# Smaller pieces for the adjacency loads and a new order of the drain in a fused graph-attention layer

## The chip, the core and the metric

The kernel runs on one core of one Trainium2 chip. The metric is the time of the whole program on the device in microseconds (us). Most executions of one kernel lie within about 1 us of its median here; the "span" in a profile is the time from the first to the last recorded instruction of one execution and is about 2 us shorter than the time of that execution on the device.

Engine names in the profile: PE is TensorE (matrix products), PEld its weight loads, DVE VectorE, ACT ScalarE, POOL GpSimd, SP SyncE. The granted clock is the share of its full clock that TensorE had, 1.00 being full; the DMA share is the mean busy share of the core's 16 DMA engines. A "q" behind a name (POOLq, SPq) marks an instruction of that engine's sequencer: a wait, a branch, the issue of a DMA.

## The reference, cut to what matters

One graph-attention layer over 4096 nodes with 4 heads, a residual and a layer norm:

```python
ht  = (x @ W).reshape(N, 4, 512).transpose(1, 0, 2)
e   = leaky_relu(src[:, :, None] + dst[:, None, :], 0.01) + adj[None]
att = softmax(e, axis=-1)
x   = layernorm(x + mean_over_heads(att @ ht))
```

The values of `adj` run up to 1e9, so in nearly every row the softmax puts all its weight on the column of the row's largest `adj`. The kernel uses this: it finds that column, gathers that row of `x`, multiplies it by the mean of the heads' weights, adds the residual and normalises. It also counts the rows in which the largest value does not lead by enough (a bound on the attention logits decides). If the count, the "flag", is not zero, a general path runs. Here it is zero, but every engine must load the flag and branch on it at the end.

## The kernel before

The 4096 rows are 32 blocks of 128 rows. A block passes these stages: load 2 MB of `adj`; largest value of each 64-column segment on VectorE; best segment, gather of it (`lead`), column within it; gather of the rows of `x` (`y`); turning (four transposes) on TensorE, a copy on ScalarE (`yt`), four products with `w_sum`; statistics on ScalarE (the reciprocal of the deviation on GpSimd) and scaling on ScalarE. In the profiles each of the four products, and a residual, shows as two matmul records (x8, x2), and the four transposes of a turning as x4. In the code below, `...` marks what is cut.

```python
def load_adj(ib):                       # SyncE's queue
    ...
    n = PIECES if ib in (0, NB - 1) else 1          # PIECES = 4
    for k in range(n):
        nc.sync.dma_start(t[:, ts(k, N // n)], adj_rows[ib][:, ts(k, N // n)])

def segment_maxima(ib, lo, hi):
    ...
    n = PIECES if ib in (0, NB - 1) else 2
    for k in range(lo * n // PIECES, hi * n // PIECES):
        nc.vector.tensor_reduce(seg_of[ib][:, ts(k, S // n)], adj_t[ib][:, ts(k, N // n)]..., op=OP.max)
```

The end of the program, the "drain", by its calls (the stores on SyncE's queue are cut; `LAST_X` is 28, `NB` 32, `FINISH` 6):

```python
find_column(NB - 2)
find_column_in_row(NB - 1)              # search over 4096 columns, then gather of row 31
rstd(slice(NB - FINISH, NB - FINISH + 2))   # GpSimd: statistics of blocks 26, 27
...
project(NB - 3, residual=False)         # turn 29, copy, four products
finish(NB - FINISH); finish(NB - FINISH + 1)
for ib in range(LAST_X, NB):
    row_norm(ib)                        # ScalarE: squares of blocks 28..31
finish_last(NB - 4, True)
find_inner(NB - 1)
bound(0)                                # largest square; TensorE turns that column
project(NB - 2, residual=False)
finish_last(NB - 3, True)
bound(1)
project(NB - 1)
finish_last(NB - 2, True)
bound(2); test(); pg = count()
finish_last(NB - 1, False)
store(nc.scalar, NB - 1, 1)
report(pg)                              # writes the flag
```

Each engine runs its instructions in this order. `finish_last` is a chain of VectorE instructions, with one small ScalarE instruction in it, over a block of 128 x 512.

## Time and profile before

| | before |
|---|---|
| time, median (lowest to highest) | 258.02 us (257.52 to 258.42) |
| span of the profiled run | 255.2 us |
| all DMA engines full | until about 236 us |
| VectorE through with block 31 of adj | 218.58 us |
| products of block 28 start | 220.22 us |
| last row of the result ready | 247.78 us |
| flag ready | 248.13 us |

The page's first part gives busy time, share of the span and number of instructions of each engine; the line of GB/s gives what the DMA engines moved in each of 40 equal slices (6.4 us each):

```profile
PE 206.2 (81%) x677; PEld 104.4 (41%) x678; DVE 188.9 (74%) x298; ACT 110.1 (43%) x266; POOL 97.5 (38%) x213
GB/s 245 433 419 424 412 420 419 429 409 411 434 414 410 417 424 417 416 419 417 414 428 406 426 409 424 417 415 412 426 412 422 413 399 403 392 379 397 47 48 46
```

No compute engine is busy all the time, and the DMA moves some 415 GB/s through nearly all slices but stops three slices before the end. Thus two limits follow one another: the loads, and a tail of dependent work.

### The profile page before, as it was taken

What the parts mean: (1) busy time and instruction counts of PE and PEld (TensorE: products, weight loads), DVE (VectorE), ACT (ScalarE), POOL (GpSimd) and SP (SyncE); (2) the same over time, 40 slices, a digit from 0 to 9 for tenths busy, and PEclk for the clock granted to TensorE, in tenths of its full rate; (3) what the DMA queues carried; (4) which work ended last, traced back from release to release, by engine and by line L of the source; (5) the groups of instructions that cost most, each with busy time, mean ns of one, the idle gap of its engine ahead of it and who ended that gap; (6) DMA issues with size and microseconds to landing.
All of it is one profiled execution on the core that took longest, in us unless ns stands there. A gap on an engine that the chain in (4) does not pass through costs nothing.

```text
span 255.2 us, 2524 instructions
## 1 busy us (share of the span) xinstructions
PE 206.2 (81%) x677; PEld 104.4 (41%) x678; DVE 188.9 (74%) x298; ACT 110.1 (43%) x266; POOL 97.5 (38%) x213
## 2 busy tenths in 40 slices
PE   0189958999999999999795979694999699684940
PEld 0035426555556665565342434242344244241410
DVE  2536686595999599959897998599959999737350
ACT  2012004044646575757481638190558182825100
POOL 1112323245445544553444445534554455530000
PEclk9999799599999999999998899998699999898895
DMA  7999999999999999999999999999999999999111
GB/s 245 433 419 424 412 420 419 429 409 411 434 414 410 417 424 417 416 419 417 414 428 406 426 409 424 417 415 412 426 412 422 413 399 403 392 379 397 47 48 46
DMA packets 15428, 97.76 MB, mean 383 GB/s; under 512 B 2344, under 2 KB 2344, under 8 KB 10032
## 3 DMA queue, kind: packets, MB, share of 16 engines
q1 hardware_dynamic: 11664, 87.82, 83.8%
q0 software_dynamic: 3584, 9.44, 9.5%
q10 hardware_dynamic: 160, 0.28, 0.3%
q8 instruction: 7, 0.11, 0.2%
q14 instruction: 13, 0.11, 0.1%
HBM read 89.15 MB, written 8.39 MB: 382 GB/s over the span
## 4 chain that ended last, share of the span: by engine, by line
DMA 32%; POOL 19%; issue 19%; PE 15%; DVE 7%; ACT 3%; SPq 1%; POOLq 0%; DVEq 0%
DMA adj_t<-in_adj_dram 14%; DMA hold<-in_x_dram 12%; PE o L211 10%; POOL y L174 6%; POOL lead L164 6%; DVE seg L151 4%; DMA hold<-in_L_gnn_W_dram 4%; DMA lead<-in_adj_dram,row 3%; POOL sd L229 3%; PE o L207 2%; POOL row L162 1%; PE pv L281 1%; ACT sq L218 1%; POOL start L169 1%; ACT hold L234 1%
## 5 line engine op out<-in xcount | busy, mean ns | idle before, releaser
L151 DVE TENSOR_REDUCE seg<-adj_t 128x32 f32<-128x2048 f32 (+1 forms) x68 | 145.9, 2150 | 36.6 <-DMA adj_t<-in_adj_dram 35.9
L211 PE MATMUL o<-w_sum,yt 128*128 128x512 f32 x256 | 125.0, 633 | 2.3 <-ACT yt L205 2.3
L211 PEld LDWEIGHTS o<-w_sum,yt 128*128 128x128 f32 x256 | 49.3, 202 | 65.3 <-issue 51.5
L174 POOL DMA_INDIRECT y<-in_x_dram,col x32 | 32.1, 1003 | 19.3 <-POOL col L187 15.5
L205 ACT COPY yt<-tp 128x512 f32<-128x512 f32 x32 | 18.8, 586 | 46.3 <-PE tp L203 46.3
L164 POOL DMA_INDIRECT lead<-in_adj_dram,row x32 | 31.0, 968 | 15.5 <-POOL row L162 15.5
L207 PE MATMUL o<-hold,ident 128*128 128x512 f32 x58 | 32.5, 645 | 0.8 <-DMA hold<-in_x_dram 0.8
L257 PE MATMUL o<-hold,ident 128*128 128x512 f32 x32 | 18.4, 726 | 16.9 <-DMA hold<-in_L_gnn_W_dram 16.9
L203 PE MATMUL tp<-ident,y 128*128 128x128 f32 x128 | 20.2, 282 | 13.9 <-DMA y<-in_x_dram,col 13.7
L203 PEld LDWEIGHTS tp<-ident,y 128*128 128x128 f32 x128 | 14.9, 144 | 25.9 <-issue 25.9
L162 POOL TENSOR_TENSOR row<-at,first 128x1 uint32<-128x1 uint32 x32 | 5.9, 184 | 50.9 <-DVE at L160 49.7
L234 ACT ACTIVATE hold<-o,nm,sd 128x512 f32<-128x512 f32 x28 | 20.3, 780 | 10.9 <-POOL nm L230 10.9
L275 ACT COPY wt<-tp 128x512 f32<-128x512 f32 x16 | 9.2, 587 | 35.4 <-PE tp L273 35.4
L187 POOL TENSOR_TENSOR col<-start,within 128x1 uint32<-128x1 uint32 x31 | 5.8, 188 | 40.4 <-DVE within L185 38.1
L281 PEld LDWEIGHTS pv<-at_d,wt 128*128 128x128 f32 x128 | 17.2, 200 | 7.4 <-ACT wt L275 3.7
L218 ACT ACTIVATE sq<-hold 128x512 f32<-128x512 f32 x32 | 19.8, 619 | 0.0
L225 ACT ACTIVATE sq<-o,nm 128x512 f32<-128x512 f32 x28 | 19.2, 688 | 0.9
L257 PEld LDWEIGHTS o<-hold,ident 128*128 128x128 f32 x32 | 7.2, 237 | 25.4 <-POOL row L162 11.6
L223 ACT ACTIVATE sq<-o 128x512 f32<-128x512 f32 x28 | 16.9, 605 | 0.0
L258 ACT ACTIVATE w_sum<-o 128x512 f32<-128x512 f32 x4 | 2.4, 598 | 33.0 <-PE o L257 33.0
L281 PE MATMUL pv<-at_d,wt 128*128 128x2 f32 x128 | 16.0, 249 | 0.6 <-ACT wt L275 0.6
L273 PEld LDWEIGHTS tp<-ident,hold 128*128 128x128 f32 x64 | 7.9, 142 | 6.9 <-issue 6.9
(73 smaller groups left out, 117.2 us busy)
## 6 DMA issues: line engine op xcount, KB each, us to landing
adj_t<-in_adj_dram SPq DMA_DIRECT2D x30, 2048.0 KB, 32.1
hold<-in_x_dram SPq DMA_DIRECT2D x8, 1024.0 KB, 33.2
out_dram<-hold SPq DMA_DIRECT2D x31, 256.0 KB, 5.2
adj_t<-in_adj_dram SPq DMA_DIRECT2D x8, 512.0 KB, 6.7
hold<-in_L_gnn_W_dram SPq DMA_DIRECT2D x4, 1024.0 KB, 18.0
lead<-in_adj_dram,row POOLq DMA_INDIRECT x32, 6.7
y<-in_x_dram,col POOLq DMA_INDIRECT x32, 8.3
out_dram<-hold ACTq DMA_DIRECT2D x1, 256.0 KB, 2.1
```

What stands on the lines that cost most here:

```text
L151: nc.vector.tensor_reduce(seg_of[ib][:, ts(k, S // n)], adj_t[ib][:, ts(k, N // n)].rearrange("p (s e) -> p s e", e=E), axis=AX.X, op=OP.max,)
L164: nc.gpsimd.indirect_dma_start(out=lead, out_offset=None, in_=adj_segs, in_offset=bass.IndirectOffsetOnAxis(ap=row[:, :1], axis=0),)
L174: nc.gpsimd.indirect_dma_start(out=y, out_offset=None, in_=x, in_offset=bass.IndirectOffsetOnAxis(ap=col[:, :1], axis=0),)
L203: nc.tensor.transpose(tp[:, kb, :], y[:, ts(kb, P)], ident)
L205: nc.scalar.copy(yt, tp)
L207: nc.tensor.matmul(o, ident, hold[:, ib, :], start=True, stop=False)
L211: nc.tensor.matmul(o, yt[:, kb, :], w_sum[:, kb, :], start=(kb == 0 and not residual), stop=(kb == KB - 1),)
L218: nc.scalar.activation(sq, hold[:, ib, :], AF.Square, accum_out=xx[:, ib : ib + 1])
L225: nc.scalar.activation(sq, o, AF.Square, bias=nm[:, i], accum_out=sd[:, i])
L234: nc.scalar.activation(hold[:, ib, :], o_ps.pop(ib), AF.Identity, bias=nm[:, i], scale=sd[:, i])
L257: nc.tensor.matmul(o, ident, hold[:, w_at + kb * H + h, :], start=(h == 0), stop=(h == H - 1))
L281: nc.tensor.matmul(pv[:, kb, h : 2 * H : H], wt[:, k, :], at_d[:, k, h : 2 * H : H], start=(k == 0), stop=(k == KB - 1),)
```

## The change

Its intent: let VectorE start on half a block instead of waiting for a whole one, and shorten the tail by giving each engine's queue an order in which nothing stands behind a wait that it does not need. The diff, cut to its core:

```diff
+    LATE = NB - Q
+    def pieces(ib):
+        return PIECES if ib == 0 or ib >= LATE else PIECES // 2
     def load_adj(ib):
-            n = PIECES if ib in (0, NB - 1) else 1
+            n = pieces(ib)
     def segment_maxima(ib, lo, hi):
-        n = PIECES if ib in (0, NB - 1) else 2
+        n = pieces(ib)
 ... (project() becomes turn(), residual(), products(ib, lo, hi); the loop's order is unchanged)
     find_column(NB - 2)
+    rstd(slice(NB - FINISH, NB - FINISH + 2))
     find_column_in_row(NB - 1)
-    rstd(slice(NB - FINISH, NB - FINISH + 2))
-    project(NB - 3, residual=False)
+    turn(NB - 3)
+    products(NB - 3, 0, KB - 1)
     finish(NB - FINISH)
     finish(NB - FINISH + 1)
-    for ib in range(LAST_X, NB):
+    for ib in range(LATE, NB):
         row_norm(ib)
+    turn(NB - 2)
+    products(NB - 3, KB - 1, KB)
+    bound(0)
+    products(NB - 2)
     finish_last(NB - 4, True)
     find_inner(NB - 1)
-    bound(0)
-    project(NB - 2, residual=False)
+    bound(1)
     finish_last(NB - 3, True)
-    bound(1)
-    project(NB - 1)
+    bound(2)
+    test()
+    turn(NB - 1)
+    residual(NB - 1)
+    products(NB - 1, 0, KB - 1)
+    pg = count()
+    products(NB - 1, KB - 1, KB)
     finish_last(NB - 2, True)
-    bound(2)
-    test()
-    pg = count()
+    report(pg)
     finish_last(NB - 1, False)
     store(nc.scalar, NB - 1, 1)
-    report(pg)
```

(The stores on SyncE's queue are cut here; they keep their order. `LATE` is 28, as `LAST_X` was. A DMA packet of adj is one row's part of a piece: 16,384 B for whole blocks, 8,192 for halves, 4,096 for quarters.)

## The prediction

> **What bounds the kernel now.** I read the slices first, then busy times in stretches, then the end in order of time. The stretches (length, busy microseconds of each engine, granted clock, DMA share, GB/s):
>
> ```profile
> 20.00:190.00 170.00, 153.23 (x541) 81.49 (x540) 137.64 (x209) 81.83 (x196) 75.87 (x160) 0.94 1.01 418
> 222.00:236.00 14.00, 9.50 (x25) 4.13 (x24) 7.88 (x13) 5.72 (x16) 2.37 (x5) 0.87 1.03 388
> 236.00:248.20 12.20, 9.60 (x26) 4.08 (x24) 5.95 (x22) 1.38 (x4) 0.00 (x0) 0.92 0.13 47
> 248.20:255.30 7.10, 0.00 (x0) 0.00 (x0) 0.00 (x0) 0.00 (x0) 0.00 (x0) 0.51 0.13 47
> ```
>
> Until 236 us the sixteen DMA engines are full (share 1.01 to 1.03) and set the pace. Then come 12 us with DMA nearly idle, in which TensorE works 9.6 us, and 7 us in which no engine computes. So there are three terms: when VectorE is through with the last block of adj (set by DMA), the drain from there to the last row, and the exit.
>
> Term one. VectorE waits for adj 35.9 us in all, and in the timeline starts a block when the whole of it has landed:
>
> ```profile
> 190.12 2.29 DVE L151 TENSOR_REDUCE seg<-adj_t 128x32 f32<-128x2048 f32 x1 [2.49 <-DMA adj_t<-in_adj_dram]
> ...
> 218.36 0.22 DVE L160 FIND_INDEX8 at<-top,seg 128x8 uint32<-128x64 f32 x1
> ```
>
> The trace's landings for blocks 27 to 30 are 190.09, 195.82, 201.41 and 207.20; the reductions start at 190.12, 195.84, 201.43 and 207.23. Block 31 comes in quarters, the last at about 213.3 (worked out from 208.59 for the first and 211.84 for the third). VectorE is one block behind, ending at 218.58.
>
> Term two, from the timeline of the end:
>
> ```profile
> 220.22 5.40 PE L211 MATMUL o<-w_sum,yt 128*128 128x512 f32 x8 [0.97 <-ACT yt L205]
> 226.13 0.94 POOL L174 DMA_INDIRECT y<-in_x_dram,col  x1 [3.81 <-PE tp L203]
> 228.45 1.45 ACT L234 ACTIVATE hold<-o,nm,sd 128x512 f32<-128x512 f32 x2 [1.77 <-POOL nm L230]
> 233.58 0.27 PE L308 MATMUL px<-ident,xm 128*1 128x128 f32 x1 [3.15 <-DVE xm L306]
> 234.98 5.20 PE L211 MATMUL o<-w_sum,yt 128*128 128x512 f32 x8 [0.68 <-ACT yt L205]
> 245.49 0.70 DVE L243 BATCH_NORM_STATS2 st<-o 128x6 f32<-128x512 f32 x1 [1.30 <-PE o L211]
> ```
>
> GpSimd stands at the gather of block 31's row until the 4.42 us search is over, then does the statistics of blocks 26 and 27 behind it; ScalarE finishes those at 228.45 and squares four rows; VectorE takes the largest at 233.36; and TensorE, at whose queue's head stands the turning of that column (the "last factor", the bound), idles 3.15 us. Row 30 had landed at 226.82, so block 30 waits for nothing of its own. After the pause its products take 5.20 us instead of 3.68.
>
> Term three. The last row is written at 247.78, the flag at 248.13, the last record ends at 255.2. The sequencers' records after the flag (count: shortest/median/longest ns, first to last start):
>
> ```profile
> L60 POOLq TENSOR_LOAD <-any_bad x1: 492/492/492, 248.2 to 248.2; - x1
> L61 PEldq COMPARE_BRANCH x2: 95/1834/3574, 248.8 to 249.2; - x2
> L641 POOLq DRAIN x3: 40/107/5307, 249.1 to 254.9; - x3
> ```
>
> All five engines load the flag at 248.2. TensorE's branch then takes 3.57 us (to 252.8), GpSimd's first drain 5.31 us (to 254.4). SyncE waits for the last store (landed at 249.88) and is through at 251.5. So the exit hangs on the flag, not on the store, by about 3 us.
>
> **What the Trainium skill says.** "DMA: Bandwidth & Descriptors", Why small descriptors are slow, gives every packet a fixed overhead of about 3 cycles. The trace agrees in kind: median 621 ns for 16,384 B, 316 for 8,192 B, 164 for 4,096 B (16 KB as 621, 632, 656). Its Anatomy of one DMA has about 2 us of fixed cost, mostly the receipt; the last store took 2.07 us. "TensorE: Matmul & The Clock Gate", What's actually happening: an idle window of about 3.4 us brings the clock to half. The trace's clock records show 0.5 from 234.6 to 238.0, after the 3.15 us pause. "Advanced Engine Details and Errata", Control Flow Timing, puts a compare-and-branch at about 108 ns; one here took 3,574 ns, so the measured one is used.
>
> **The change part by part.**
>
> *adj in halves and quarters.* Bytes are the same. Cost: halves need 8 more packets on each engine in a block (128 rows over 16 engines), and two of 8,192 B take 2 x 316 - 621 = 11 ns more than one of 16,384 B: 8 x 11 = 0.09 us a block, 27 blocks, 2.4 us by the medians. From 20 to 60 us the medians were 619 and 312, giving 8 x 5 ns x 27 = 1.1 us. I take 1.7, and 0.2 more for quarters of block 28 on: adj lands some 1.9 us later. Gain: VectorE has block 27's first half done when the second lands (190.09 + 1.9 = 192.0), ends that block 2.27 + 0.55 us later at 194.8, and then works through four blocks at 5.75 us each (its time for block 31 before, 212.81 to 218.58): 194.8 + 23.0 = 217.8 to 218.0, against 218.58. Quarters land every 1.4 us and take 1.15 us, so VectorE no longer waits for whole blocks. Net: -0.6 us. In flight are now eight pieces of 1 or 0.5 MB instead of whole blocks; each piece waits for the eighth before it. 4 MB at 410 GB/s is 10 us of work, so I expect no hole.
>
> *Drain.* Let T be the start of block 28's products, 220.22 before and 219.6 after.
> - T to T+5.4: products of 28, as slow as before (the clock dropped at 221.0 after waits that stay).
> - Turning and copying 29: T+6.6. Three products at 0.92: T+9.35. Turning 30 (0.6): T+9.95. Fourth product: T+10.85.
> - ScalarE: copy of 29 to T+6.55, blocks 26 and 27 finished (1.45; their statistics now precede the gather on GpSimd) to T+8.0, four squares (2.44) to T+10.45, copy of 30 to T+11.05. VectorE's largest value is there at T+10.65, before TensorE asks: the 3.15 us are gone.
> - Products of 30 at full clock (3.7): T+14.8, against T+19.96 before (240.18). That is 5.2 us.
> - Bound 0.3, turning 31 0.6, copy 0.65, three products 2.75, count 0.2, fourth product 0.92: T+20.3.
> - VectorE: block 28 from T+10.65 (2.75 us as before), two small ones 0.5, block 29 2.75, factor and test 1.3, block 30 2.75: T+20.7. Report 0.45, flag at T+21.1. Block 31's statistics and scaling 2.3 (245.49 to 247.78): T+23.4.
> Before, the last row stood at T+27.56. The drain gives 4.2 us; VectorE, not TensorE, is then last by 0.7.
>
> *Exit.* Flag T+21.1: GpSimd 0.95 to its drain and 5.3 in it, T+27.35. VectorE needs 3.9 us from its last instruction to its own drain (248.13 to 252.0, load and branch within), T+27.3. Store: 2.1 landing, 0.3, then 1.3 in SyncE: T+27.1. All meet; 0.8 us of closing gives T+28.2. After the last row that is 4.8 instead of 7.4: 2.6 us.
>
> Sum: 0.6 + 4.2 + 2.6 = 7.4 us. 258.02 - 7.4 = 250.6; I put it at 250.8 because the chains meet tightly.
>
> **The rivals.**
> (1) Smaller pieces slow the DMA by more. For: steady means are 627 and 324 ns, which gives 8 x 21 ns x 27 = 4.5 us instead of 1.7. Against: from 20 to 60 us, with 512 packets of 8,192 B among 700 of 16,384 B, the core moved 421 GB/s, more than anywhere else. It would make 253.5.
> (2) GpSimd's long drain or the branches are a fixed tail after the last work, not after the flag. For: the drain stands near the end whatever runs. Against: it starts 0.2 us after its branch, while a store is still out. It would leave 7.4 us of exit: 253.3.
> (3) The clock. Fuller work before 219 us could spare the slow products of 28 (1.6 us): 249.1. Or a new short wait throttles 30 or 31 again: 252.3.
> (4) The eight in flight are too few and leave holes in the DMA. For: the queue shrinks from some 10 to 4 MB. Against: stores of 256 KB, eight in flight, still moved 388 GB/s. It could cost 3 us or more.
> (5) The row gathers gain, since each waits behind shorter packets (8.3 us landing under whole blocks, 6.0 among stores). They are on no path that I found in the middle; up to 1 us in the drain.
>
> **Range and chances.** (1) and (2) are each some one in six and cost about 2.7 us; both together cancel most of the gain. (3) is worth 1.5 us either way. The range is 248.6 to 253.6. Two per cent is 252.86, 2 us above my middle, so faster has 0.8. Slower needs holes: 0.02.
>
> **What would show it.** Right: adj's last landing near 215, VectorE through block 31 by about 218; no wait of TensorE for the largest square; products of 30 near 3.7 us; the flag before the last row; under 5 us from the last row to the end; full DMA to about 238. Wrong: DMA slices under full before 230, a last landing past 217, a wait of over 1 us between the products of 29 and 31, or GpSimd's drain still ending 6 us after the last row.

## The result and the profile after

| | before | after |
|---|---|---|
| time, median of the first job | 257.77 us (4 runs) | 249.25 us (4 runs, 248.82 to 250.11) |
| ratio | | 0.9673, 95% interval 0.9635 to 0.9711 |
| span | 255.2 us | 246.9 us |

A ratio here is the mean time of one kernel's fast runs over that of the other's of the same rounds, so it is not quite the ratio of the medians. In the experiments the profiled run counts in the medians and not in the ratio; in the first job it counts in both.

The stretches of the changed kernel (start:end, length, busy us and number of instructions of PE, PEld, DVE, ACT and POOL, granted clock, DMA share, GB/s); the third ends with the last row:

```profile
20.00:190.00 170.00, 153.81 (x551) 81.01 (x550) 135.87 (x206) 82.08 (x197) 76.39 (x160) 0.96 1.02 412
222.00:236.00 14.00, 13.09 (x41) 5.84 (x40) 8.43 (x20) 6.64 (x18) 2.83 (x5) 1.00 1.04 392
236.00:241.70 5.70, 3.27 (x9) 0.95 (x7) 4.68 (x15) 0.59 (x2) 0.00 (x0) 1.00 0.75 286
241.70:246.90 5.20, 0.00 (x0) 0.00 (x0) 0.00 (x0) 0.00 (x0) 0.00 (x0) 0.60 0.19 65
```

The profile is that of the fastest of the four runs (248.82 us). The first row is the cost: with a DMA share that is still full, 412 GB/s instead of 418. The second is the gain: TensorE works 13.1 of 14 us where it had worked 9.5, at full clock. The stretch after the last row, with no engine computing, is 5.2 us long where it was 7.4.

VectorE's timeline in the changed kernel:

```profile
193.13 2.29 DVE L155 TENSOR_REDUCE seg<-adj_t 128x32 f32<-128x2048 f32 x1 [0.53 <-DMA adj_t<-in_adj_dram]
196.00 2.33 DVE L155 TENSOR_REDUCE seg<-adj_t 128x16 f32<-128x1024 f32 x2
...
219.09 0.23 DVE L164 FIND_INDEX8 at<-top,seg 128x8 uint32<-128x64 f32 x1 [0.29 <-issue]
```

The first line is the second half of block 27. VectorE waited for it, so it landed at 193.13; all of block 27 had landed at 190.09 before. The loads are 3.0 us late by then. From 196.0 on VectorE works without waiting and is through with block 31 at 219.32, 0.74 us later than before. So the earlier start on each block did not make up for the slower loads.

The end, in order of time, for the same instructions as in the prediction:

```profile
220.46 3.70 PE L217 MATMUL o<-w_sum,yt 128*128 128x512 f32 x8 [1.71 <-ACT yt L206]
...
223.80 0.19 POOL L236 TENSOR_TENSOR nm<-nm,sd 128x2 f32<-128x2 f32 x1
...
225.54 1.46 ACT L240 ACTIVATE hold<-o,nm,sd 128x512 f32<-128x512 f32 x2
...
229.70 0.27 PE L314 MATMUL px<-ident,xm 128*1 128x128 f32 x1
...
229.96 3.70 PE L217 MATMUL o<-w_sum,yt 128*128 128x512 f32 x8
...
239.42 0.68 DVE L249 BATCH_NORM_STATS2 st<-o 128x6 f32<-128x512 f32 x1
```

The statistics of blocks 26 and 27 are ready at 223.99 (before, 228.42), ScalarE finishes the two blocks 2.9 us earlier, and the turning of the column of largest squares has no wait in brackets any more. The products of block 30 take 3.70 us and start 5.0 us earlier than before. The products of block 28 also take 3.70 us, where they took 5.40.

The sequencers at the end of the changed kernel:

```profile
L60 POOLq TENSOR_LOAD <-any_bad x1: 503/503/503, 239.5 to 239.5; - x1
L61 PEldq COMPARE_BRANCH  x2: 95/1954/3814, 240.1 to 240.6; - x2
L656 POOLq DRAIN  x3: 40/107/5307, 240.4 to 246.6; - x3
L656 SPq DRAIN  x3: 7/7/7, 246.0 to 246.3; - x3
```

The flag is loaded at 239.5, before the last row is ready (241.69). GpSimd's drain, again 5,307 ns, ends at 245.8, and SyncE, which waits for the last stores, is through at 246.0. The two paths now meet.

### The profile page after: what moved, and what is told of

Its sections match the earlier page's. It is cut to its first block, busy times and chain, and to the rows that moved or that the text cites. A ratio compares the mean times of both kernels' runs of the same rounds, so it can differ in the third digit from the quotient of the medians.

```text
span 246.9 us, 2569 instructions
## 1 busy us (share of the span) xinstructions
PE 201.8 (82%) x677; PEld 101.2 (41%) x678; DVE 188.8 (76%) x304; ACT 109.6 (44%) x266; POOL 97.5 (39%) x213
## 4 chain that ended last, share of the span: by engine, by line
DMA 47%; issue 19%; POOL 19%; DVE 10%; ACT 2%; POOLq 0%; PE 0%; DVEq 0%
DMA adj_t<-in_adj_dram 38%; DMA hold<-in_L_gnn_W_dram 6%; POOL lead L168 6%; POOL y L178 6%; DVE seg L155 4%; DMA y<-in_x_dram,col 3%; POOL sd L235 2%; POOL start L173 1%; POOL row L166 1%; DVE st L249 1%; POOL col L191 1%; DVE hold L255 1%; ACT sq L224 1%; DVE hold L246 1%; POOL sd L234 1%
## 5 line engine op out<-in xcount | busy, mean ns | idle before, releaser
L217 PE MATMUL o<-w_sum,yt 128*128 128x512 f32 x256 | 118.4, 604 | 7.4 <-ACT yt L206 7.4
L217 PEld LDWEIGHTS o<-w_sum,yt 128*128 128x128 f32 x256 | 46.2, 191 | 65.7 <-issue 45.5
L263 PE MATMUL o<-hold,ident 128*128 128x512 f32 x32 | 22.2, 860 | 16.3 <-DMA hold<-in_L_gnn_W_dram 16.3
L210 PE MATMUL o<-hold,ident 128*128 128x512 f32 x58 | 30.6, 610 | 0.0
L204 PE MATMUL tp<-ident,y 128*128 128x128 f32 x128 | 20.2, 281 | 11.3 <-DMA y<-in_x_dram,col 11.2
L263 PEld LDWEIGHTS o<-hold,ident 128*128 128x128 f32 x32 | 8.5, 279 | 27.2 <-POOL row L166 11.5
L287 PEld LDWEIGHTS pv<-at_d,wt 128*128 128x128 f32 x128 | 16.3, 191 | 6.8 <-ACT wt L281 3.7
L287 PE MATMUL pv<-at_d,wt 128*128 128x2 f32 x128 | 15.3, 244 | 0.6 <-ACT wt L281 0.6
```

The lines of the kernel that those rows point to most:

```text
L204: nc.tensor.transpose(tp[:, kb, :], y[:, ts(kb, P)], ident)
L210: nc.tensor.matmul(o_ps[ib], ident, hold[:, ib, :], start=True, stop=False)
L217: nc.tensor.matmul(o_ps[ib], yt_of[ib][:, kb, :], w_sum[:, kb, :], start=(start and kb == 0), stop=(kb == KB - 1),)
L263: nc.tensor.matmul(o, ident, hold[:, w_at + kb * H + h, :], start=(h == 0), stop=(h == H - 1))
L287: nc.tensor.matmul(pv[:, kb, h : 2 * H : H], wt[:, k, :], at_d[:, k, h : 2 * H : H], start=(k == 0), stop=(k == KB - 1),)
```

## The experiments

Three theories had to be told apart. A: the gain is the drain's order and the flag's place, and the smaller pieces give nothing or cost. B: the pieces carry a good part. C, on the exit: it is a fixed tail after the last work. All twelve kernels gave correct results. "Before" ran beside each of them; its median was 257.90, 258.01 and 257.58 us in the three jobs. The jobs ran on different chips (e1 to e4, e5 to e8, and e9 to e12), so runs of different jobs are compared by their ratios.

| run | what | median us | ratio to before, 95% interval |
|---|---|---|---|
| e9 | the changed kernel again | 249.06 | 0.9685 (0.9652 to 0.9717) |
| e1 | before + pieces | 256.37 | 0.9984 (0.9941 to 1.0027) |
| e2 | changed, whole blocks | 247.69 | 0.9610 (0.9587 to 0.9634) |
| e3 | changed, flag last | 251.79 | 0.9776 (0.9747 to 0.9805) |
| e4 | changed, whole to 27, then quarters | 248.70 | 0.9641 (0.9612 to 0.9669) |
| e5 | changed, whole to 23, halves to 27, quarters | 247.27 | 0.9590 (0.9548 to 0.9633) |
| e6 | changed, statistics behind the gather | 252.19 | 0.9791 (0.9747 to 0.9836) |
| e7 | changed, 30 turned after the bound's column | 250.64 | 0.9722 (0.9681 to 0.9763) |
| e8 | e2 + statistics ahead in the whole loop | 247.40 | 0.9608 (0.9560 to 0.9656) |
| e10 | e5 + e8 | 249.83 | 0.9686 (0.9642 to 0.9729) |
| e11 | before + flag early | 256.47 | 0.9951 (0.9923 to 0.9980) |
| e12 | changed, every block in quarters | 254.18 | 0.9866 (0.9829 to 0.9903) |

### e1: the pieces alone

```diff
+    def pieces(ib): return PIECES if ib == 0 or ib >= LATE else PIECES // 2
-            n = PIECES if ib in (0, NB - 1) else 1      # and 2 in segment_maxima
+            n = pieces(ib)
```

> The kernel before with adj in halves and the last four blocks in quarters, nothing else. Theory A (the pieces buy nothing: shorter packets make the last adj land 2.6 us later, 215.4 instead of 212.8, and VectorE ends block 31 at 219.3 instead of 218.6): 257.8 to 258.8 us, ratio 1.000 to 1.004, with the 3.15 us wait of TensorE for the largest square still there. Rival B (the pieces carry a good part of the 8.5 us, by fuller TensorE work and no drop of its clock before the drain): under 256.3 us, with the products of block 28 at 3.7 us instead of 5.4. If only the clock counts and it is luck of the window, the time follows that one group: 1.7 us less where it shows 3.7.

The median was 256.37 us, but the runs spread from 254.85 to 259.24, and the ratio cannot be told from 1. So A's range of times (257.8 to 258.8) was missed, and B's was not reached. That ratio counts two runs that the record marks slow (258.70 and 259.24); the other three of its rounds give 0.994. By the packet records the last adj was in at 215.29, against 212.75 before; VectorE was through with block 31 at 218.68, not at the 219.3 expected. TensorE still waited for the largest square:

```profile
232.68 0.27 PE L312 MATMUL px<-ident,xm 128*1 128x128 f32 x1 [2.37 <-DVE xm L310]
```

Its profiled run (254.85) was the fastest and had the products of blocks 28 and 30 at 3.70 us each, without a drop of the clock. B's limit, 256.3 us, is a ratio of 0.994, just at the interval's lower end, so a gain of about 1.5 us in the old drain, of pieces or of the clock, is not ruled out. It is no large part of 8.5 us.

### e2: the changed kernel with whole blocks

```diff
-            n = pieces(ib)
+            n = PIECES if ib in (0, NB - 1) else 1      # and 2 in segment_maxima
```

> The changed kernel with adj as before (whole blocks, 0 and 31 in quarters). Theory A: 248.2 to 249.3 us, as fast as the changed kernel or up to 1 us faster: last adj back at 212.8, DMA done 2.6 us earlier, block 31 through VectorE at 218.6. Rival B (the pieces carry part of the gain): over 250.5 us.

It was faster than the changed kernel: 247.69 us, and its interval (0.9587 to 0.9634) lies under that of the changed kernel run again (0.9652 to 0.9717). Theory A holds, by somewhat more than its best case. The loads moved as fast as before again:

```profile
20.00:190.00 170.00, 148.53 (x545) 78.41 (x544) 136.86 (x210) 83.03 (x197) 76.58 (x160) 0.98 1.01 418
```

VectorE was through with block 31 at 218.23, the last row stood at 240.70, and the products of 28 began at 219.88:

```profile
219.88 3.70 PE L217 MATMUL o<-w_sum,yt 128*128 128x512 f32 x8 [1.30 <-ACT yt L206]
```

So the pieces cost the changed kernel some 0.75% (0.9685 - 0.9610), or about 1.9 us.

### e3: the flag last

```diff
-    report(pg)
     finish_last(NB - 1, False)
     store(nc.scalar, NB - 1, 1)
+    report(pg)
```

> The changed kernel with the flag reported after the last row, as before. Theory A (the exit hangs on the flag: 1 us to GpSimd's drain, 5.3 us in it): exit from the last row's end back from 5.2 to about 7.4 us, 251.2 to 251.6 us. Rival (the exit is a fixed tail after the last work or store): 249.0 to 249.5 us.

It took 251.79 us, just over A's range, about 0.9% or 2.4 us more than the changed kernel by the ratios (0.9776 - 0.9685). The last row came at 241.85, nearly as in the changed kernel (241.69), but the exit after it took 7.44 us instead of 5.22:

```profile
L60 POOLq TENSOR_LOAD <-any_bad x1: 502/502/502, 242.3 to 242.3; - x1
L656 POOLq DRAIN  x3: 40/107/5307, 243.2 to 249.0; - x3
```

The long drain starts 0.9 us after the flag's load, wherever the flag is, and sets the end. Theory C falls.

### e4: whole blocks, then quarters

```diff
-            n = pieces(ib)
+            n = PIECES if ib == 0 or ib >= LATE else 1
```

> The changed kernel with whole loads for blocks 1 to 27 and quarters for 28 to 31. Theory A: packets of 16,384 B bring the last adj back to about 213.2; but VectorE, which starts block 27 when all of it has landed (190.1) and takes 5.1 us for it and 5.8 us for each block in quarters, still ends at about 218.4: 248.3 to 249.2 us. Rival B: over 250.5 us.

It gave 248.70 us, as A expected, and was no faster than e2 (247.69). The last adj was in at 212.90, VectorE through at 218.48. Whole loads through block 27 restore the DMA, but since block 27 must land whole, VectorE gains nothing from the quarters. In its profiled run the products of block 28 were slow:

```profile
219.81 5.40 PE L217 MATMUL o<-w_sum,yt 128*128 128x512 f32 x8 [2.36 <-ACT sq L224]
```

### e5: whole, then halves, then quarters

```diff
-        return PIECES if ib == 0 or ib >= LATE else PIECES // 2
+        if ib == 0 or ib >= LATE: return PIECES
+        return PIECES // 2 if ib >= LATE - Q else 1
-        n = pieces(ib)                  # in segment_maxima
+        n = max(2, pieces(ib))
```

> The changed kernel with whole loads for blocks 1 to 23, halves for 24 to 27, quarters for 28 to 31. If what the pieces cost is their packets (8 ns each) and what they give is an earlier start of VectorE on the last blocks, both show here: last adj near 213.3 (0.6 us later than with whole blocks), block 31 through VectorE at 216 to 217 instead of 218.2. If the start of block 28's products hung on VectorE, 246.5 to 247.5 us; if it hangs on ScalarE's chain (statistics of 24 and 25, then 26, then the copy of 28), which starts from VectorE's end of block 30, the same, for that comes earlier too. Rival (neither counts): 247.7 as with whole blocks.

It reached 247.27 us, the lowest median of all. The last adj was in at 213.81, and VectorE was through 2.6 us earlier than in the changed kernel:

```profile
190.58 2.29 DVE L157 TENSOR_REDUCE seg<-adj_t 128x32 f32<-128x2048 f32 x1 [0.21 <-DMA adj_t<-in_adj_dram]
...
216.45 0.23 DVE L166 FIND_INDEX8 at<-top,seg 128x8 uint32<-128x64 f32 x1 [0.29 <-issue]
```

Products of 28 began at 217.91 and the last row stood at 239.56, 2.1 us before the changed kernel's. In this profile the pieces pay, since they shorten the wait that lasts to the end. About half a microsecond of it went in a longer exit (5.7 us: SyncE was held by the stores until 243.1, 3.5 us after the last row; in the changed kernel it was 3.0), and the interval overlaps that of e2, so the gain over whole blocks is not certain. It does beat both kernels: its interval ends at 0.9633, that of e9 begins at 0.9652.

### e6: the statistics behind the gather again

```diff
     find_column(NB - 2)
-    rstd(slice(NB - FINISH, NB - FINISH + 2))
     find_column_in_row(NB - 1)
+    rstd(slice(NB - FINISH, NB - FINISH + 2))
```

> The changed kernel with the statistics of blocks 26 and 27 on GpSimd behind the gather of block 31's row again. Theory A (this order is half of the drain's gain: the four squares and the largest square hang on it): the statistics at about 226.7 instead of 222.7, the blocks finished at 228 instead of 225.5, squares to 231.7, largest square at 232, so TensorE waits about 2 us before block 30's products and the time is 251 to 252 us. Rival (the gain is TensorE's order alone, turning 30 before the bound): 249.3 to 249.8 us.

It took 252.19 us, just over A's range, about 1.1% or 2.7 us more than e9's ratio, and the wait was back:

```profile
228.61 0.20 POOL L236 TENSOR_TENSOR nm<-nm,sd 128x2 f32<-128x2 f32 x1
```

```profile
233.00 0.27 PE L314 MATMUL px<-ident,xm 128*1 128x128 f32 x1 [1.38 <-DVE xm L312]
```

The statistics were 4.8 us later than in the changed kernel. The wait was 1.38 us and not 2; products of block 28 were slow in this profile (5.22 us), which hid part of it. One line's place on GpSimd is a third of the whole gain.

### e7: block 30 turned after the bound's column

```diff
-    products(NB - 3, 0, KB - 1)
+    products(NB - 3)
 ...
-    turn(NB - 2)
-    products(NB - 3, KB - 1, KB)
     bound(0)
+    turn(NB - 2)
```

> The changed kernel with all four products of block 29 in one, and block 30 turned after the bound's column, as before. Theory A: with the statistics early the largest square comes at 229.5, 0.7 us after block 29's products end, so the wait is only about 0.7 us, and turning and copying 30 (1.2 us) now stands behind it: 0.7 to 1.3 us more than the changed kernel, 250.2 to 250.9 us. Rival (turning 30 inside 29's products is what takes the 3.15 us away): over 252 us.

It took 250.64 us, 0.4% or about 1 us more than e9's ratio; the intervals overlap slightly. The wait stayed small:

```profile
230.26 0.27 PE L314 MATMUL px<-ident,xm 128*1 128x128 f32 x1 [0.30 <-DVE xm L312]
```

So the turning inside block 29's products hides about one turn and copy. What took the 3.15 us wait away is the earlier statistics (e6), not TensorE's order.

### e8: the statistics ahead in the whole loop

```diff
+        if pair: rstd(slice(t - FINISH, t - FINISH + 2))
         find_segment(t)
-        if pair: rstd(slice(t - FINISH, t - FINISH + 2))
```

> Whole blocks as in e2, and on GpSimd the statistics of a pair ahead of the search and gather for the block at hand, in the whole loop. In e2 block 28's copy waits for ScalarE, which finishes 24 and 25 late since their statistics stand behind block 30's gather. Theory: finished by 215 instead of 217.5, copy of 28 at about 218.7, products of 28 at 219.3 instead of 219.9; 246.9 to 247.5 us. Rival (GpSimd then waits for ScalarE and the gathers come later): 247.7 us or more.

The median was 247.40 us, but the ratio (0.9608) is that of e2 (0.9610). The mechanism came about: products of block 28 began at 218.41 instead of 219.88. The gain was then lost to the next wait, the gather of block 30's row:

```profile
227.46 0.63 PE L204 MATMUL tp<-ident,y 128*128 128x128 f32 x4 [1.39 <-DMA y<-in_x_dram,col]
```

The last row came at 240.44, only 0.26 us earlier than in e2.

### e9: the changed kernel again

> The changed kernel itself, to stand beside the next ones in the same rounds: 249.2 to 249.7 us.

It took 249.06 us, ratio 0.9685, with the same picture: VectorE through at 219.00, products of 28 from 220.32 in 3.70 us, exit 5.13 us.

### e10: e5 and e8 together

> The loads of e5 (whole to 23, halves to 27, quarters to 31) with e8's statistics ahead of the search: VectorE through block 31 at 216.6, products of 28 no longer behind ScalarE's chain. If the start of 28's products counts: 217.2 instead of 217.9, 246.3 to 247.0 us. If the stores that are still leaving (last one at 239.5 us in e5) set the end, no better than e5: 247.2.

This was a miss: 249.83 us, from 247.82 to 251.11, slower than either part. The start did not come as forecast either: in its profiled run (250.61) VectorE was through with block 31 at 218.24 instead of 216.6, and the products of 28 began at 218.15. The last row was ready at 239.47, only 0.1 us before e5's, and the exit took 9.1 us. SyncE's waits between 205 us and the end (in all, how often, longest):

```profile
SPq L260 <- DMA out_dram<-hold: 6.4, 3, 5.9
```

Its last store was issued only at 242.16, since it waited for an earlier store's completion, and its own last packets left after 245. While it waited, the engines that had branched fetched instructions: the records show 16,384-byte instruction packets of 1.3 and 1.6 us at 239.2 and 242.8. I suspect that these hold up a store on one DMA engine, but no run isolates it. The last adj packet (215.34) was also later than in e5, for a reason that I did not find.

### e11: the flag early, alone

```diff
+    report(pg)
     finish_last(NB - 1, False)
     store(nc.scalar, NB - 1, 1)
-    report(pg)
```

> The kernel before with the flag reported ahead of the last row's statistics, nothing else. The count stands behind the last product, so the flag comes at 246.1 instead of 248.1 and the last row 0.5 us later, at 248.3. GpSimd's drain then ends at 252.4, the store's path at about the same time: 1.7 to 2.1 us less, 255.7 to 256.1 us. Rival (fixed tail): 258.3 us.

The exit shrank as expected (5.12 us in the profile, after a last row at 247.63):

```profile
L60 POOLq TENSOR_LOAD <-any_bad x1: 507/507/507, 245.5 to 245.5; - x1
L641 POOLq DRAIN  x3: 40/107/5307, 246.4 to 252.5; - x3
```

But the rounds give 0.5% or 1.3 us (0.5 to 2.0), less than the 1.7 to 2.1 that I expected. The direction holds and the size is short. In the changed kernel the flag's place was worth 2.4 us (e3). The profiles do not explain the difference: in both kernels the flag then leads the last row by 2.2 us and the exits are 5.1 to 5.2 us.

### e12: every block in quarters

```diff
-        return PIECES if ib == 0 or ib >= LATE else PIECES // 2
+        return PIECES
```

> The changed kernel with every block of adj in quarters: the same bytes in packets of 4,096 B. If smaller packets are what the pieces cost (316 ns for 8,192 B, 164 for 4,096 B, so 16 packets more on each engine in each of 27 blocks at some 8 to 12 ns), the last adj lands 3.5 to 5 us after 215.4, VectorE ends block 31 at 222 to 224 and the time is 252 to 254 us. Rival (the pieces' cost is the eight in flight or chance): either unchanged at 249.5, or DMA slices well under full.

It took 254.18 us, just over the expected range. The same bytes in 4,096-byte packets moved more slowly still, with the DMA engines as full:

```profile
20.00:190.00 170.00, 148.49 (x540) 78.07 (x540) 138.97 (x254) 81.37 (x196) 74.52 (x155) 0.98 1.03 404
```

The last adj came in at 220.89, 5.5 us after the changed kernel's 215.38. Against halves, quarters add 16 packets to each engine in each of 27 blocks: 5.5 us / 432 = 12.7 ns a packet. With halves the rate is about the same: 3.0 us / (27 x 8) = 14 ns. (The last landing of one kind of loads varies by up to 1.2 us between the profiles, so neither figure is sharper than a few ns.) It is the packet that costs, and the queue of only eight pieces in flight leaves no holes.

## Why the prediction was right, and where it was not

The prediction said 250.8 us and 248.6 to 253.6; the result was 249.25. The mechanisms of the drain and the exit were right; that of the adj pieces was not. The total came so near partly by luck: in the profile, 1.7 us of the drain's gain came from the clock, which the sum had not counted, and made up for the two terms that fell short. Its terms, measured on the spans (8.3 us in all, against 7.4 in the sum):

| term | predicted | measured |
|---|---|---|
| start of block 28's products | -0.6 us | +0.2 us |
| drain, from there to the last row | -4.2 us | -6.3 us |
| exit after the last row | -2.6 us | -2.2 us |
| sum | -7.4 us | -8.3 us |

**adj in pieces: the sign was wrong, through a mis-sized term.** The step "11 ns more ... 2.4 us by the medians", lowered to 1.7 us for block 27 (1.9 with the quarters), should have been 3.0 us. The rest of that step was close: it let VectorE take 2.27 + 0.55 us for the second half and 23.0 to 23.2 us for four blocks, which from 193.13 gives 218.95 to 219.15, and it finished at 219.32. (The prediction also put the quarters' 0.2 us already on block 27, which comes before them, and had worked out 213.3 for the last landing before, which the packet records put at 212.75; nothing rests on either.) The error came from taking medians. A queue that is always full adds up mean durations, and the packet records between 60 and 120 us have means of 627.4 ns for 16,384 B (before) and 320.2 ns for 8,192 B (after): 2 x 320.2 - 627.4 = 13 ns, times 8 packets and 27 blocks, is 2.8 us. Rival (1) saw the danger, but took its 4.5 us from the means of other loads (x), which are longer. e2 and e12 show the cost, e12 with a larger dose.

**The waits removed.** "VectorE's largest value is there ... before TensorE asks: the 3.15 us are gone" held in every kernel with the statistics ahead, but for 0.30 us in e7, and e6 brings a wait back. With the wait went the half clock of block 30's products, which took 5.20 us before and 3.70 after. The times relative to the products of 28 also held once the clock of block 28 is allowed for: the products of 30 started at T+9.5, which with the 1.7 us that block 28 saved is T+11.2, against T+11.1 predicted. The flag came at T+19.0, likewise T+20.7 against 21.1, and the last row at T+21.2, T+22.9 against 23.4.

**The clock.** The step that failed in the drain is "products of 28, as slow as before". They took 3.70 us. Rival (3) had this case at 249.1 us. Of the fourteen profiles, the products of 28 were slow (5.2 to 5.4 us) in before, e4, e6, e11 and e12, and full in the other nine, with and without pieces. The clock records of the traces show what goes with it. In all fourteen the clock changes only at the ends of stretches of 3.413 us, and these lie differently in each execution: one begins at 218.9 us in the changed kernel's profile and at 219.9 in e9, the same kernel. In the five slow cases TensorE was busy (by records whose ends are partly modelled) in 31 to 45% of the stretch before the drop (44% before, 31% in e4); in the other nine, no stretch over the same wait had less than 48% (e9). It is no sharp limit: e1 kept full clock after a stretch of 41% at 228.9. So this 1.7 us belongs to where the stretches happened to lie against the wait, rather than to the change, as far as these runs can tell. Shorter waits leave less to chance: an estimate that slides such a stretch over the wait finds less than 45% busy in about a quarter of the positions in the profile of before and a third in e9's (none in the first profile of the same kernel), and in none in those of e2, e5 and e8. The spread of e1's six runs, 4.4 us, fits this: the two slowest had a mean granted clock of 0.936 and 0.929, the fastest 0.953. Which of their products were slow is not recorded.

**The exit.** "The exit hangs on the flag, not on the store" is confirmed by e3 (7.44 us again) and in direction by e11. The exit was 0.4 us longer than predicted: the last store's completion came at about 244.4, some 2.7 us after its issue at 241.72, and not 2.1. By the packet records the last store's packets took 1.7 us from its issue in the three profiles with the flag last (before, e1, e3), and 1.9 to 2.2 us in the eleven with the flag early. In the eleven, a 16,384-byte instruction packet of 0.9 to 1.3 us ran at the same time; in the three it came after the store. That fits the suspicion told under e10, that engines which branch early fetch instructions in the way of a store; no run isolates it. "All meet" was right: GpSimd's drain ended 0.25 us before SyncE's.

**Its own signs.** Two of the "right" signs failed: VectorE was through at 219.32, not by about 218, and the exit took 5.2 us, not under 5. None of the "wrong" signs came.

**Rivals (2) and (4).** The fixed tail is refuted by e3. Holes through too few pieces in flight did not occur: the DMA share stayed at 1.02, and at 1.03 with quarters.

**What the parts are worth** in the changed kernel, each by the ratio of the run without it to 0.9685: statistics ahead 1.1% (e6), flag early 0.9% (e3), block 30 inside 29 0.4% (e7), pieces -0.75% (e2). They need not add up, since each shifts which wait ends last, and they make about half of the 3.2% in all. The earlier bound, test and count were not taken back on their own, so what they give is not shown.

## What to carry to other kernels

In an in-order queue, ask of every instruction what it makes those behind it wait for: moving three tiny instructions in front of one gather was worth 2.7 us here (e6), and a flag that all engines branch on should be ready well before the last result. When the DMA engines are full, splitting loads costs by the packet, so leave most of them whole and, if at all, split the last ones, where the earlier start reaches the end (e5; in e4, with only the last four split, nothing was gained). For a resource that is always full, estimate with mean durations, not medians.

## What the Trainium skill lacked or had wrong

- "DMA: Bandwidth & Descriptors", Bandwidth, advises to batch DMAs to at least 1 MiB. Pieces of 1 MiB, in place of 2 MiB, still cost here: 412 GB/s instead of 418, 13 to 14 ns for each packet more. The page gives no time for one packet more where packets have 4,096 to 16,384 B and all engines are full.
- "Advanced Engine Details and Errata", Control Flow Timing, has about 108 ns for a compare-and-branch. TensorE's branch on the flag took 3,574 ns before and 3,814 ns after; 95 ns was measured for its other one. The section has no slow case, and no page that I found gives a time for one. Before, this branch (to 252.8 us) still ended ahead of GpSimd's drain (254.4).
- "VectorE: DVE Perf Modes", The DRAIN you can't avoid, calls the drains at a program's start and end boilerplate of about 12 ns. GpSimd's first drain after the branch took 5.3 us in all fourteen profiles, and it set the end of the kernel before. No page that I found tells of it.
- "TensorE: Matmul & The Clock Gate", What's actually happening, has half clock after at least one idle window of about 3.4 us. Here no idle window was needed: block 28's products ran at half clock after stretches of 3.413 us in which TensorE was busy for 31 to 45%. Pauses of 2.90 us (e11) and 3.15 us (before) were followed by half clock too, one of 2.37 us (e1) by full.
